# A graph layer on one core: the row that places and bins are compared with moves into a PSUM bank, and the counts get one PSUM buffer in place of two

## The chip, the cores and the metric

The kernel runs on one core of one Trainium2 chip. The metric is the device time of one execution in microseconds (us), the median of the runs shown. The engines are called PE (TensorE, matmuls; PEld is its weight load), DVE (VectorE), ACT (ScalarE), POOL (GpSimd) and SP (SyncE, which here only issues DMAs). SBUF is the on-chip memory of all engines, PSUM the memory in which PE leaves its sums[...].

## The reference

There are 12,500 nodes with 128 features and 400,000 edges, each with a source `src`, a destination `dst` (the edges are sorted by it), 20 attributes and a weight.

```
smu(v) = ((1 + a) * v + (1 - a) * v * erf(mu * (1 - a) * v)) / 2      a = 0.01, mu = 2.5

h    = relu(layernorm(x))
hf   = h @ W_in2f.T
Wij  = (smu(f_ij @ W_f1.T + b_f1) @ W_f2.T + b_f2) * edge_weight
x_ij = hf[dst] * Wij
agg  = segment_sum(x_ij, src, 12500)
out  = x + smu(agg @ W_o1.T + b_o1) @ W_o2.T + b_o2
```

So every edge reads the row of its destination, multiplies it with a filter made from its attributes, and is added to the row of its source. The sources are in no order.

## The kernel before

**Tiles.** The edges are cut into 3125 tiles of 128, four tiles make a group (782 groups; `GRP`), two groups share one set of loads (`load`, L366). The nodes are cut into `NB` = 98 bins of 128 by their source number. The groups come in seven parts (`PARTS`): six of 118 groups and one of 74. Each part has a buffer `buf` in HBM in which every bin has a fixed number of places.

**One group on its way.** PE multiplies the attributes with `w_f1` into `pu` (`hide`, L478), ACT applies Gelu (`ge`, L486), DVE makes `sm` of it (L494), PE multiplies with `w_f2` into `pw` (L528). DVE compares the edges' destinations with the partition number (`oh`, L386), and with this one-hot matrix PE gathers the destinations' rows from `hw` into `ph` (L509); ACT copies them to `hg` (L517), DVE multiplies `pw` and `hg` into `mt` (L538). PE turns `mt` into `pt` (L548), ACT scales it with the edge weight into the message buffer `ms` (L558, four instructions), of which there are six, and POOL stores the 128 rows of each tile into `buf` with one indirect DMA (L561): four for a group, 3125 in all. A buffer `ms` comes free when its stores have landed.

**Where a row goes.** The store needs each edge's place in its bin. `bins` (L392) has DVE compare the row 0, 1, 2, ... with the edges' bin numbers `hi_b`, giving `po` (128 edges x 4 tiles x 98 bins, L399), and add up the earlier tiles' in `co` (L410, L413). `count` (L419) has PE sum these down the edges into `pc` (L426, L427), and `read` (L447) has ACT pick each edge's number out of `pc` (L456, four instructions and their sums). `number` (L465) makes the index `ix` that the store uses.

**Adding up.** While a part is stored, the part before it is summed: SP loads places of two bins at a time into `rw` (L582), `choose` (L586) has DVE compare the row 0, 1, 2, ... with the number inside the bin that each place carries, giving the one-hot matrix `se` (128 places x 12 x 128, L593), and `add` (L597) has PE multiply it with the places into `pg` (L606), which DVE adds to `agg` (L619). The last part is summed after the last store, together with the output layers (`half`, L320, and `rest`, L332). Part 0 has nothing to sum; in its place the remaining node rows are normed and multiplied with `w_in` (`rows_of_h`, L185).

**The order.** In the loop over groups (L678) the order on PE, DVE, ACT and SP is the order in which the lines stand (`manual_schedule`): in the round of group g the steps `turn(g)`, `send(g)`, `number(g+1)`, `weigh(g+1)`, `gather(g+1)`, `take(g+1)`, half of the sums, `mix(g+1)`, `hide(g+2)`, `bend(g+2)`, `count(g+2)`, `read(g+2)`, `smooth(g+2)`, every other round `pick`, `bins(g+3)`, and the rest of the sums. Nobody overtakes on an engine. The sums begin in the fifth round of a part (`WAIT` = 4), and `choose` for the first bins stands before the third.

The row 0, 1, 2, ... is kept twice in SBUF: `irow` as float32, made by POOL (L113), and `irow_b` as bfloat16, copied from it (L116). PSUM is full in the loop: two buffers each for `pc` and `pg`, one each for `pu`, `ph`, `pw` and `pt`.

Of the kernel before, what the change touches and what calls it, by code (L numbers as in the profile page):

```python
# [9 lines left out]
F32 = mybir.dt.float32  # L10
BF = mybir.dt.bfloat16
# [8 lines left out]
P = 128  # L20
# [9 lines left out]
GRP = 4  # L30
# [9 lines left out]
def gnn_kernel(  # L40
# [19 lines left out]
    nc = tc.nc  # L60
# [4 lines left out]
    NB = (N + P - 1) // P  # L65
# [10 lines left out]
    for n in PARTS:  # L76
        n = min(n, left)
# [7 lines left out]
    for a, n in eps_of:  # L85
# [9 lines left out]
    const = ctx.enter_context(tc.tile_pool(name="const", bufs=1))  # L95
# [17 lines left out]
    irow = const.tile([P, P], F32, name="irow")  # L113
    nc.gpsimd.iota(irow, pattern=[[1, P]], base=0, channel_multiplier=0,
                   allow_small_or_imprecise_dtypes=True)
    irow_b = const.tile([P, P], BF, name="irow_b")  # L116
    nc.vector.tensor_copy(irow_b, irow)

    tri = const.tile([P, P], F16, name="tri")
    lift = const.tile([P, P], F32, name="lift")  # L120
# [97 lines left out]
    with tc.tile_pool(name="prep", bufs=1) as prep, \  # L218
# [44 lines left out]
        for a, m in chunks(NT // P, GRP) + [(NT // P, 0)]:  # L263
# [8 lines left out]
            elif NT % P:  # L272
                m = NT % P
# [71 lines left out]
    with tc.tile_pool(name="ld", bufs=4) as ld, \  # L345
# [4 lines left out]
            tc.tile_pool(name="ps2", bufs=2, space=PSUM) as ps2, \  # L350
            tc.tile_pool(name="ps1", bufs=1, space=PSUM) as ps1, \
            tc.manual_schedule(engines={ET.PE, ET.DVE, ET.Activation, ET.SP}):
        NF = 4
        fbufs = []
        for i in range(NF):
            fb = ld.tile([P, SUP * P], F32, name=f"f{i}", bufs=1)
# [9 lines left out]
        def load(s):  # L366
# [3 lines left out]
            e0, n = t0 * P, nt * P  # L370
            fb = fbufs[s % NF]
            nc.sync.dma_start(fb[0:R, :n], f_t[:, e0:e0 + n])
# [19 lines left out]
        def bins(g):  # L392


            if g >= NG:
                return
            t, n = groups[g]
            po = cnt.tile([P, GRP, NB], F16, name="po")
            nc.vector.tensor_tensor(po[:, :n], irow_b[:, :NB].unsqueeze(1).to_broadcast([P, n, NB]),  # L399
                                    hi_b[:, t:t + n].unsqueeze(2).to_broadcast([P, n, NB]), op=ALU.is_equal)  # L400
            co = cnt.tile([P, GRP + 1, NB], F16, name="co")
            if g in first:
                k = first[g]
                nc.vector.memset(co[:, 0], 0.0)
                m = sum(groups[i][1] for i in range(g, min(g + eps_of[k][1] * PER, NG)))
                begins[k] = (t, cnt.tile([P, max(n for _, n in eps_of) * SUP], F32, name="hic", bufs=2))
                nc.vector.tensor_scalar(begins[k][1][:, :m], hi_b[:, t:t + m], float(CAP[k]), None, op0=ALU.mult)
            else:
                pl, cl, nl = last.pop(0)
                nc.vector.tensor_add(co[:, 0], cl[:, nl - 1], pl[:, nl - 1])  # L410
            more = g + 1 in first or g + 1 in (NG, BY)
            for j in range(1, n + more):
                nc.vector.tensor_add(co[:, j], co[:, j - 1], po[:, j - 1])  # L413
            last[0] = (po, co, n)
            bins_of[g] = (po, co)
# [3 lines left out]
        def count(g):  # L419

            if g >= NG:
                return
            n = groups[g][1]
            po, co = bins_of.pop(g)
            pc = ps2.tile([P, GRP, NB], F32, name="pc")
            nc.tensor.matmul(pc[:, :n], ones_h, co[:, :n], start=True, stop=False)  # L426
            nc.tensor.matmul(pc[:, :n], tri, po[:, :n], start=False, stop=True)  # L427
            counts[g] = pc
            if g + 1 == BY:
                pt = ps1.tile([P, GRP * P], F32, name="ph")[:, :NB]  # L430
                nc.tensor.matmul(pt, ones_h, co[:, n], start=True, stop=True)
                mm = cnt.tile([P, 2], F32, name="mm")
                nc.vector.tensor_reduce(mm[:, 0:1], pt[:, :NB - 1], op=ALU.max, axis=AX.X)
                nc.vector.tensor_scalar(bad[:, 3:4], mm[:, 0:1], float(ZMIN[0]), None, op0=ALU.is_gt)
            if g + 1 in first or g + 1 == NG:

                k = epoch[g // PER]
                pt = ps1.tile([P, GRP, P], F32, name="ph")[:, 0, :NB]
                nc.tensor.matmul(pt, ones_h, co[:, n], start=True, stop=True)
                mm = cnt.tile([P, 2], F32, name="mm")  # L440
                nc.vector.tensor_reduce(mm[:, 0:1], pt, op=ALU.max, axis=AX.X)
                nc.vector.tensor_reduce(mm[:, 1:2], pt[:, :NB - 1], op=ALU.min, axis=AX.X)
                i = 4 + 2 * k
                nc.vector.tensor_scalar(bad[:, i:i + 1], mm[:, 0:1], float(CAP[k]), None, op0=ALU.is_gt)
                nc.vector.tensor_scalar(bad[:, i + 1:i + 2], mm[:, 1:2], float(ZMIN[k]), None, op0=ALU.is_lt)
# [140 lines left out]
        def choose(k, c):  # L586

            b = c * SPAN[k]
            if b >= NB:
                return  # L590
            m = min(SPAN[k], NB - b) * Q[k]
            se = rowp.tile([P, ROWS, P], F32, name="se", bufs=2)
            nc.vector.tensor_tensor(se[:, :m], irow.unsqueeze(1).to_broadcast([P, m, P]),  # L593
                                    rows_in[c][:, :m, P:P + 1].to_broadcast([P, m, P]), op=ALU.is_equal)
            sel[c] = se

        def add(k, b, q):  # L597

            g = b % GRP
            c, i = b // SPAN[k], b % SPAN[k]  # L600
            if q == 0 and g == 0:
                pgs[0] = ps2.tile([P, GRP, P], F32, name="pg")
            if q == 0 and i == 0:
                choose(k, c + 1)
            o = i * Q[k] + q
            nc.tensor.matmul(pgs[0][:, g, :], rows_in[c][:, o, 0:P], sel[c][:, o, :], start=(q == 0),  # L606
                             stop=(q == Q[k] - 1))
            if q < Q[k] - 1:
                return
            if i == SPAN[k] - 1 or b == NB - 1:  # L610
                rows_in.pop(c), sel.pop(c)
                fetch(k, c + AHEAD)
            if g == GRP - 1 or b == NB - 1:
                dst = agg[:, (b - g) * P:(b + 1) * P]
                src = pgs[0][:, :g + 1].rearrange("p b n -> p (b n)")
                if k == 0:
                    nc.vector.tensor_copy(dst, src)
                else:
                    nc.vector.tensor_add(dst, dst, src)  # L619
# [18 lines left out]
        for g in range(3):  # L638
            bins(g)
        count(0)  # L640
        read(0)
        count(1)
        read(1)
        number(0)
# [33 lines left out]
        for g in range(NG):  # L678
# [24 lines left out]
            if k and i == WAIT - 2:  # L703
                choose(k - 1, 0)
# [14 lines left out]
            hide(g + 2)  # L719
            bend(g + 2)  # L720
            count(g + 2)
            read(g + 2)
            smooth(g + 2)
            if g % PER == 0:
                pick((g + 4) // PER)
            bins(g + 3)
            parts(k - 1, hi)
            step()
            assert k == 0 or next(h_steps, None) is None
        k = EPOCHS - 1  # L730
        begin(k)
        choose(k, 0)
        mids, ends = [], []
        units_in = {}
# [169 lines left out]
```

## Time and profile before

| what | value |
|---|---|
| median of 3 runs | 4601.06 us (4593.67 to 4603.17) |
| the profiled execution, its own time | 4605.67 us |
| its span, from the first to the last instruction | 4603.9 us |
| mean granted clock of PE | 0.949 |
| DVE, `se` (L593), 128x1536 | 326 instructions, 1753 ns each |
| DVE, `po` (L399), 128x392 | 781 instructions, 559 ns each |
| DVE, `mt` (L538), 128x512 | 781 instructions, 748 ns each |
| ACT, reads of `pc` (L456) | 3125 instructions, 361 ns each, and as many of 226 ns that take the sums out |
| PE, sums of rows (L606) | 7840 instructions, 1109 us busy |
| first and last store (L561) | from 93.6 us; the last begins at 4405.8 us |

A group's row in the profile gives the line, the engine, the operation, what it writes and reads, and the number of instructions; then the busy time in us and the mean of one in ns; then the engine's idle time just before them and what ended most of it. A row of the timeline gives the start and the duration in us, the same names, and in square brackets the idle time before it with what ended it. A row of a wait gives who waited for whom: us in total, times, the longest. A float32 matmul shows as two instructions on PE. A stretch given in us counts from the start of the span.

### The profile page before, as it was taken

What the parts mean: (1) busy time and instruction counts of PE and PEld (TensorE: products, weight loads), DVE (VectorE), ACT (ScalarE), POOL (GpSimd) and SP (SyncE); (2) the same over time, 40 slices, a digit from 0 to 9 for tenths busy, and PEclk for the clock granted to TensorE, in tenths of its full rate; (3) what the DMA queues carried; (4) which work ended last, traced back from release to release, by engine and by line L of the source; (5) the groups of instructions that cost most, each with busy time, mean ns of one, the idle gap of its engine ahead of it and who ended that gap; (6) DMA issues with size and microseconds to landing.
All of it is one profiled execution on the core that took longest, in us unless ns stands there. A gap on an engine that the chain in (4) does not pass through costs nothing. (4 is left out here: it accounts for less than half of the span.)

```text
span 4603.9 us, 73307 instructions
## 1 busy us (share of the span) xinstructions
PE 3824.8 (83%) x18332; PEld 2340.7 (51%) x18596; DVE 3181.2 (69%) x8458; ACT 2809.9 (61%) x11054; POOL 3355.9 (73%) x3137
## 2 busy tenths in 40 slices
PE   4777787988879888879888878888798888799967
PEld 2334434555545555545555545555455555466656
DVE  5876676767667667757766767667576676687746
ACT  3776785666656666657666666666576666566500
POOL 1777777777777777777777777777777777777720
PEclk9999998999999999989999989999999999899978
DMA  6945565656646656646655556556465555466556
GB/s 187 212 139 169 157 167 173 193 174 184 181 131 214 190 175 183 181 145 206 190 180 172 168 171 199 172 179 186 125 209 173 169 172 166 138 197 183 164 179 175
DMA packets 457331, 808.84 MB, mean 176 GB/s; under 512 B 82228, under 2 KB 258630, under 8 KB 456512
## 3 DMA queue, kind: packets, MB, share of 16 engines
q1 hardware_dynamic: 328136, 573.65, 43.1%
q0 software_dynamic: 101504, 212.48, 14.2%
q10 hardware_dynamic: 27256, 17.94, 1.3%
q8 instruction: 147, 2.41, 0.2%
q14 instruction: 288, 2.36, 0.2%
HBM read 449.68 MB, written 354.07 MB: 175 GB/s over the span
## 5 line engine op out<-in xcount | busy, mean ns | idle before, releaser
L561 POOL DMA_INDIRECT buf<-ms,ix x3125 | 3349.1, 1072 | 1050.3 <-issue 268.7
L558 ACT ACTIVATE ms<-pt,w_sb 128x128 f32<-128x128 f32 x3125 | 903.2, 386 | 905.8 <-DMA buf<-ms,ix 699.8
L606 PEld LDWEIGHTS pg<-se,rw 128*128 128x128 f32 x7840 | 1087.1, 195 | 189.9 <-issue 51.7
L606 PE MATMUL pg<-se,rw 128*128 128x128 f32 x7840 | 1109.0, 278 | 35.7 <-DVE se L593 35.6
L456 ACT ACTIVATE jk<-pc,nbig 128x98 f32<-128x98 f32 x3125 | 1034.8, 361 | 12.3 <-PE pc L427 11.9
L548 PE MATMUL pt<-ident,mt 128*128 128x128 f32 x3125 | 512.8, 288 | 561.3 <-DVE mt L538 558.1
L528 PE MATMUL pw<-sm,w_f 128*128 128x512 f32 x1564 | 923.5, 674 | 27.1 <-DVE sm L494 21.6
L538 DVE SCALAR_TENSOR_TENSOR mt<-pw,b,hg 128x512 f32<-128x512 f32 x782 | 584.7, 748 | 514.6 <-ACT hg L517 511.3
L478 PE MATMUL pu<-f,w_f 128*128 128x512 f32 x1564 | 813.8, 602 | 2.6 <-DVE sm L494 2.5
L486 ACT ACTIVATE ge<-pu 128x512 f32<-128x512 f32 x782 | 472.9, 605 | 395.4 <-PE pu L478 360.2
L593 DVE TENSOR_TENSOR se<-irow,rw 128x1536 f32<-128x1536 f32 x327 | 572.6, 1751 | 193.0 <-DMA rw<-buf 159.5
L456 ACT ACTIVATION_READ_ACCUMULATOR jk<-pc,nbig 128x1 f32 x3125 | 705.0, 226 | 0.0
L548 PEld LDWEIGHTS pt<-ident,mt 128*128 128x128 f32 x3125 | 355.3, 145 | 668.5 <-DVE mt L538 664.1
L509 PE MATMUL ph<-oh,hw 128*128 128x512 bf16 (+1 forms) x2082 | 651.5, 396 | 16.1 <-issue 3.1
L494 DVE SCALAR_TENSOR_TENSOR sm<-pu,ge 128x512 f32<-128x512 f32 x782 | 535.6, 685 | 150.6 <-ACT ge L486 143.8
L517 ACT ACTIVATE hg<-ph 128x512 f32<-128x512 f32 x782 | 471.4, 603 | 210.2 <-PE ph L509 207.9
L413 DVE TENSOR_TENSOR co<-co,po 128x98 f16<-128x98 f16 x2351 | 503.7, 214 | 81.3
L509 PEld LDWEIGHTS <-hw 128*128 128x128 bf16 x2346 | 239.2, 102 | 585.9 <-issue 493.6
L399 DVE TENSOR_TENSOR po<-irow_b,hi_b 128x392 f16<-128x392 bf16 x782 | 436.8, 559 | 0.0
L555 DVE CAST ms<-lo_b 128x4 f32<-128x4 bf16 x782 | 150.6, 193 | 315.9 <-DMA buf<-ms,ix 312.8
L528 PEld LDWEIGHTS pw<-sm,w_f 128*128 128x128 f32 x1564 | 244.1, 196 | 165.7 <-DVE sm L494 163.1
L426 PE MATMUL pc<-co,ones_h 128*128 128x392 f16 x782 | 257.9, 330 | 13.3 <-DMA rbc<-rel_dram 12.8
(114 smaller groups left out, 1771.2 us busy)
## 6 DMA issues: line engine op xcount, KB each, us to landing
rw<-buf SPq DMA_DIRECT2D x326, 774.0 KB
buf<-zero SPq DMA_DIRECT2D x294, 387.0 KB
rbc<-rel_dram SPq DMA_DIRECT2D x390, 256.0 KB
buf<-ms,ix POOLq DMA_INDIRECT x3125
hw<-h_dram SPq DMA_DIRECT2D x391, 96.0 KB
f<-in_f_t SPq DMA_DIRECT2D x390, 80.0 KB
buf<-zero SPq DMA_DIRECT2D x49, 258.0 KB
h_dram<-hs SPq DMA_DIRECT2D x24, 384.0 KB
```

The costliest lines, as they stand in the source:

```text
L413: nc.vector.tensor_add(co[:, j], co[:, j - 1], po[:, j - 1])
L456: nc.scalar.activation(jk, pc[:, j], AF.Relu, bias=nbig, accum_out=sl[:, j:j + 1])
L478: nc.tensor.matmul(pu[:, :n], w_f1, loaded[g // PER][0][:, o:o + n], start=True, stop=True)
L494: nc.vector.scalar_tensor_tensor(sm[:, :n], units_of.pop(g)[:, :n], LIN, hidden[g][:, :n], op0=ALU.mult, op1=ALU.add)
L509: nc.tensor.matmul(ph[:, :n], hw[:, q * D:(q + 1) * D], oh[:, o:o + n], start=(q == 0), stop=(q == 2))
L528: nc.tensor.matmul(pw[:, :n], w_f2, hidden.pop(g)[:, :n], start=True, stop=True)
L538: nc.vector.scalar_tensor_tensor(mt[:, :n], pws.pop(g)[:, :n], b2, rows_of.pop(g)[:, :n], op0=ALU.add, op1=ALU.mult)
L548: nc.tensor.transpose(pt[:, j, :], mt[:, j * P:(j + 1) * P], ident)
L558: nc.scalar.activation(ms[:, j, 0:P], pt[:, j], AF.Copy, scale=w_sb[:, t + j:t + j + 1])
L561: i = nc.gpsimd.indirect_dma_start(out=bufs[k][:, :], out_offset=bass.IndirectOffsetOnAxis(ap=ix[:, j:j + 1], axis=0), in_=ms[:, j, :], in ...
L593: nc.vector.tensor_tensor(se[:, :m], irow.unsqueeze(1).to_broadcast([P, m, P]), rows_in[c][:, :m, P:P + 1].to_broadcast([P, m, P]), op=ALU ...
L606: nc.tensor.matmul(pgs[0][:, g, :], rows_in[c][:, o, 0:P], sel[c][:, o, :], start=(q == 0), stop=(q == Q[k] - 1))
```

## The change

The float32 row is copied once into a PSUM bank of its own (`irow_ps`), and `po` and `se` read it there. To free that bank, `pc` has one buffer in place of two, of four times 128 columns, of which 98 are used. The bfloat16 copy `irow_b` goes. The order of the steps in the loop is as before; apart from the new names and the shape of `pc`, only a few steps of the preparation trade places.

```diff
-    irow_b = const.tile([P, P], BF, name="irow_b")
-    nc.vector.tensor_copy(irow_b, irow)
...
             tc.manual_schedule(engines={ET.PE, ET.DVE, ET.Activation, ET.SP}):
+
+        irow_ps = ps1.tile([P, GRP * P], F32, name="irow_ps")[:, 0:P]
+        nc.vector.tensor_copy(irow_ps, irow)
...
             po = cnt.tile([P, GRP, NB], F16, name="po")
-            nc.vector.tensor_tensor(po[:, :n], irow_b[:, :NB].unsqueeze(1).to_broadcast([P, n, NB]),
+            nc.vector.tensor_tensor(po[:, :n], irow_ps[:, :NB].unsqueeze(1).to_broadcast([P, n, NB]),
                                     hi_b[:, t:t + n].unsqueeze(2).to_broadcast([P, n, NB]), op=ALU.is_equal)
...
-            pc = ps2.tile([P, GRP, NB], F32, name="pc")
+            pc = ps1.tile([P, GRP, P], F32, name="pc")[:, :, 0:NB]
             nc.tensor.matmul(pc[:, :n], ones_h, co[:, :n], start=True, stop=False)
...
             se = rowp.tile([P, ROWS, P], F32, name="se", bufs=2)
-            nc.vector.tensor_tensor(se[:, :m], irow.unsqueeze(1).to_broadcast([P, m, P]),
+            nc.vector.tensor_tensor(se[:, :m], irow_ps.unsqueeze(1).to_broadcast([P, m, P]),
                                     rows_in[c][:, :m, P:P + 1].to_broadcast([P, m, P]), op=ALU.is_equal)
```

## The prediction

> **What bounds the kernel now.** I read the page's busy table first, then the costliest groups, then the waits, then GpSimd's (POOL's) rows in order of time beside VectorE's (DVE's). In the table PE looks like the bound with 83%, and POOL has 73%:
>
> ```profile
> PE 3824.8 (83%) x18332; PEld 2340.7 (51%) x18596; DVE 3181.2 (69%) x8458; ACT 2809.9 (61%) x11054; POOL 3355.9 (73%) x3137
> ```
>
> The table misleads. The groups give the indirect stores 1072 ns each and 1050 us of idle time before them, and the waits say who stands behind them: ScalarE (ACT) waits 700 us for a store to land, because it wants the message buffer `ms` back.
>
> ```profile
> L561 POOL DMA_INDIRECT buf<-ms,ix x3125 | 3349.1, 1072 | 1050.3 <-issue 268.7
> ```
>
> ```profile
> ACT ms L558 <- DMA buf<-ms,ix: 699.8, 306, 20.1
> ```
>
> POOL in order of time, from 2048 us:
>
> ```profile
> 2048.62 0.96 POOL L561 DMA_INDIRECT buf<-ms,ix  x1 [0.30 <-ACT ms L558]
> 2049.89 1.69 POOL L561 DMA_INDIRECT buf<-ms,ix  x1 [0.30 <-issue]
> 2051.89 0.96 POOL L561 DMA_INDIRECT buf<-ms,ix  x1 [0.30 <-ACT jk L456]
> ...
> 2062.01 0.96 POOL L561 DMA_INDIRECT buf<-ms,ix  x1 [0.30 <-DVE co L410]
> 2063.28 1.97 POOL L561 DMA_INDIRECT buf<-ms,ix  x1 [0.30 <-issue]
> ```
>
> DVE in the same stretch:
>
> ```profile
> 2048.99 1.75 DVE L593 TENSOR_TENSOR se<-irow,rw 128x1536 f32<-128x1536 f32 x1
> ...
> 2062.67 1.75 DVE L593 TENSOR_TENSOR se<-irow,rw 128x1536 f32<-128x1536 f32 x1
> ```
>
> The reader is to see two things. First, the gap between two stores is always 0.30 us: it is the price of a step, not a wait. Over all 3125 rows only 13 us of gap lie above 0.305 us. So POOL works without a pause from 93.6 to 4406.8 us, and an undisturbed store costs 0.96 + 0.305 = 1.266 us, 5.07 us for a group of four. Second, two stores are long, and each ends 0.84 us after the end of a `se` (2048.99 + 1.75 = 2050.74, and 2049.89 + 1.69 = 2051.58; 2062.67 + 1.75 = 2064.42, and 2063.28 + 1.97 = 2065.25). A store that meets a `se` early in its life stands still until that `se` is over.
>
> I counted this over the trace. 597 of the 3125 stores are longer than 1.0 us, by 346 us in all above 0.961 us; 586 of them end 0.84 us after the end of a DVE row, to 20 ns. By that row: `se` (L593) 294 stores and 280 us, `po` (L399) 167 and 43 us, `oh` (L386) 70 and 10 us, the first `co` add (L410) 40 and 6 us, `hs` (L211) 13 and 5 us, others under 1 us. The other way round, by what DVE ran 90 ns after the start of a store: `se` held 294 of 307, `po` 179 of 202, `hs` 13 of 13; `mt` (L538) 0 of 292, `agg` (L619) 0 of 63, `sm` (L494) 10 of 432, by 0.1 us each. `se`, `po` and `hs` read two tensors of SBUF; `mt`, `agg` and `sm` read one of SBUF and one of PSUM. That is the whole of the case for the change: it turns `se` and `po` into the second kind.
>
> **The blocks: which rule.** The Trainium skill ("SBUF — State Buffer", "Who interferes with whom") says in my words that VectorE and GpSimd share one pair of SBUF ports as an exclusive lock, and that a VectorE instruction with two SBUF inputs contends with a GpSimd instruction that reads SBUF. But it goes on that tensor_tensor does not stall such stores: it takes "only the pair's read interface", and descriptors need the write interface (the page calls this inferred). By that sentence the change is worth 0 us. By the rows it is worth up to 280 + 43 = 323 us. I take the rows: 294 of 307 is no accident. (The rule is also too wide in one place: the f16 adds at L413 have two SBUF inputs and held 0 of 359.)
>
> **What is gained, part by part.** The edge groups come in seven parts of 118 groups (74 in the last), with first stores at 93.6, 726.6 and so on to 3986.6 us. POOL gains all of a block only where nothing else becomes the limit.
>
> Parts 1 to 5: `se` and `po` blocks sum to 52.4 + 55.0 + 50.3 + 55.1 + 52.7 = 265.5 us. The other engines can follow. After each part's start they run free of POOL for some twenty groups, because the message buffers are free there:
>
> ```profile
> 771.77 1.14 ACT L558 ACTIVATE ms<-pt,w_sb 128x128 f32<-128x128 f32 x4 [0.57 <-PE pt L548]
> ...
> 832.34 1.16 ACT L558 ACTIVATE ms<-pt,w_sb 128x128 f32<-128x128 f32 x4
> ```
>
> These rows are 13 groups apart: 60.6 / 13 = 4.66 us a group, against POOL's new 5.07 plus the `oh` blocks, 5.09. So 265 us.
>
> Part 0: it has no `se`. Its `po` blocks are 4.3 us before group 48 and 3.1 us after group 92. Between these, steps for the node rows slow the engines to (578.3 - 323.4) / 42 = 6.07 us a group, POOL waits for them, and 0.7 us of blocks gain nothing. So 7 us.
>
> Part 6: the same 588 sums of rows fall on 70 groups, not 114, and PE is nearly full:
>
> ```profile
> 2100.00:2600.00 500.00, 437.36 (x2133) 269.85 (x2161) 356.82 (x938) 322.37 (x1287) 389.72 (x363) 0.98 0.61 186
> 4000.00:4370.00 370.00, 349.66 (x1967) 240.44 (x2001) 294.63 (x708) 238.54 (x945) 292.62 (x255) 0.99 0.60 182
> ```
>
> (First the stretch and its length, then PE, PEld, DVE, ACT, POOL busy.) PE goes from 87% to 95%. The L558 rows of 30 groups here, from 3995.0 to 4148.9 us, give 5.13 us a group, above 5.07. POOL took 419.2 us; with 49.1 us of blocks gone it would need 370, but the engines need 71.25 x 5.13 plus two groups at 5.1, 375.7 us. So 43.5 us, and here PE is the next bound.
>
> After the last store (4406.8 us) come 197 us of sums and output in which POOL does nothing. `se` blocks nobody there, so nothing changes. Sum gained: 265.5 + 7.4 + 43.5 = 316 us.
>
> **What is added.** (a) The duration of `se` and `po`. Nearest rows: L337 adds PSUM and SBUF, 128x512, in 690 ns; L338 adds two SBUF tensors of that size in 692 ns. I take 0. Above: a row of PSUM read over and over has no row in this trace; see the rivals. Below: L619 has 683 ns, 9 ns less, x 327 = 3 us of DVE time that hides under POOL. (b) One `pc` in place of two: the count of group g+1 on PE now waits for ACT's four reads (L456) of group g, and behind it PE's sums of rows queue. In the trace the next count starts at least 1.95 us after the last of these reads (median 2.6), except once: the second count of all starts 0.97 us before. So 1 us at the start, and 0 later; the cover is the time that PE spends on `pt`, `pw`, `ph` and `pu` in between. Were the cover gone, 0.5 us a group would take 4.66 to 5.16 and cost 5 x 118 x 0.07 = 41 us. (c) `pc` is now written as four runs of 98 with gaps. The Trainium skill ("PSUM — Partial Sum Buffer", Specifications) says that a non-contiguous pattern slows matmuls significantly; no row here shows one. I take 0, since the run of 98 stays whole. Twice the price would be 0.33 us a group (L426 and L427 start 0.17 us apart): 4.99 in parts 1 to 5, still under 5.09, and 71 x 0.33 = 23 us in part 6. (d) One 128x128 copy into PSUM in place of one cast of 0.21 us; DVE then waits 1.90 us for a load anyway: 0. Moved steps in the preparation: 0, within 3 us either way. (e) At each part's start the engines' lead over POOL (from the last L558 row of a group to its first store) falls from some 23 to 2.3 us, then 4.1, 3.9; a faster POOL eats 0.3 to 0.5 us of it per group and may run dry for a moment: 6 x 0.5 = 3 us.
>
> Sum: 316 - 1 - 3 = 312 us. The profiled execution took 4605.7 us (span 4603.9 and 1.8 around it), so 4294; it lies 4.6 us above the median 4601.06, so 4289.
>
> **Rivals.** *PE binds in parts 1 to 5 too* (12%). For: PE's busy share would rise from 87% to 95%, which is where part 6 stands. At 5.2 us a group: 5 x 118 x (5.2 - 5.09) = 65 us, so 4354, up to 4390 with (c). Against: the 4.66 measured with both kinds of work running. *The change does not do what it says* (4%): the operand's place is not what blocks; then 4601. Against: 0 of 292 for `mt`. *Slower* (4%): DVE reads the repeated PSUM row at half pace. `se` would take 1.75 + 1.6 and `po` 0.56 + 0.41 us. DVE is busy 357 of 500 us, 3.9 of 5.5 us a group, and would need 3.9 + 0.67 + 0.41 = 5.0, and 0.65 us a group that it spends waiting for `hg` (511 us in all) does not shrink: 5.65 in parts 1 to 5, and 6.5 in part 6, where `se` comes more often; 94 + 118 x 5.4 + 590 x 5.65 + 74 x 6.5 + 197 and 33 x 1.6 for the tail gives 4795. It decides from about 0.5 us of added DVE time a group on.
>
> **How the numbers follow.** The likeliest case (80%) is 4289, in itself 4262 (no block at all left, 346 us, and no loss to PE but 7) to 4320 (PE's pattern cost in part 6 and a few us more). The range 4262 to 4350 takes in half of the first rival. A difference of 0.2%, 9 us, is about what a measurement of this kernel can tell. Faster 0.92, the same 0.04, slower 0.04.
>
> **What would show it.** Right: POOL's mean falls from 1072 to about 970 ns, long stores behind `se` and `po` vanish and those behind `oh` stay; `se` stays at 1.75 and `po` at 0.56 us; ACT's wait for the landing falls from 700 to about 400 us; the last store starts near 4090 us; 197 us follow it. Wrong: stores still end 0.84 us after a `se`, or gaps above 0.305 us appear in parts 1 to 5 (PE binds, and PE waits at L426 for the reads at L456), or `se` grows.

## The result and the profile after

| | before | after |
|---|---|---|
| median | 4602.11 us (4 runs, 4593.67 to 4607.44) | 4288.51 us (4 runs, 4284.47 to 4295.33) |
| the profiled execution, its own time | 4605.67 us | 4295.33 us |
| its span | 4603.9 us | 4293.6 us |
| first store begins, last store ends | 93.6, 4406.8 us | 93.5, 4095.8 us |
| after the last store | 197.1 us | 197.8 us |
| stores longer than 1.0 us | 597, by 346 us | 134, by 20 us |

The ratio is 0.9322, with a 95% interval of 0.9303 to 0.934. The whole difference lies between the first and the last store: that stretch is 311 us shorter, the span 310 us.

The first line of the busy table and the group of the stores after the change (the line numbers are one higher than before in this part of the code):

```profile
PE 3745.7 (87%) x18332; PEld 2305.2 (54%) x18596; DVE 3177.7 (74%) x8458; ACT 2825.2 (66%) x11054; POOL 3029.8 (71%) x3137
```

```profile
L562 POOL DMA_INDIRECT buf<-ms,ix x3125 | 3023.1, 967 | 1065.4 <-issue 278.4
```

DVE does the same work in the same time (3178 us, before 3181); its two changed instructions:

```profile
L594 DVE TENSOR_TENSOR se<-irow_ps,rw 128x1536 f32<-128x1536 f32 x326 | 570.6, 1750 | 162.0 <-DMA rw<-buf 135.8 <-PE pg L607 25.9 <-PE ph L510 0.2
L400 DVE TENSOR_TENSOR po<-irow_ps,hi_b 128x392 f16<-128x392 f32 x781 | 433.6, 555 | 0.0
```

POOL is shorter by 326 us in the same 3125 stores: 967 ns each in place of 1072. The gap between two stores is again 0.305 us; in parts 1 to 5, where hardly a gap is longer, POOL still sets the pace, although PE and DVE have larger shares in the table.

POOL in order of time, and below it the two `se` of DVE in the same stretch:

```profile
1947.40 1.04 POOL L562 DMA_INDIRECT buf<-ms,ix  x1 [0.30 <-ACT ge L487]
...
1950.05 0.96 POOL L562 DMA_INDIRECT buf<-ms,ix  x1 [0.30 <-issue]
1951.31 0.96 POOL L562 DMA_INDIRECT buf<-ms,ix  x1 [0.31 <-issue]
...
1960.17 0.96 POOL L562 DMA_INDIRECT buf<-ms,ix  x1 [0.30 <-issue]
1961.44 0.96 POOL L562 DMA_INDIRECT buf<-ms,ix  x1 [0.30 <-ACT jk L457]
```

```profile
1949.56 1.75 DVE L594 TENSOR_TENSOR se<-irow_ps,rw 128x1536 f32<-128x1536 f32 x1
...
1959.49 1.75 DVE L594 TENSOR_TENSOR se<-irow_ps,rw 128x1536 f32<-128x1536 f32 x1
```

The stores that begin at 1950.05 and 1960.17 us begin inside a `se`, as those of 2049.89 and 2063.28 us did before, and take 0.96 us where those took 1.69 and 1.97 us. By the same count as in the prediction (what DVE ran 90 ns after a store began): `se` held 0 of 384 stores, `po` 0 of 254; `oh` held 81 of 123, for 12 us.

### The profile page after: what moved, and what is told of

It reads as the page before. It is cut to its first block, busy times and chain, and to the rows that moved or that the text cites. A ratio compares the mean times of both kernels' runs of the same rounds, so it can differ in the third digit from the quotient of the medians.

```text
span 4293.6 us, 74022 instructions
## 1 busy us (share of the span) xinstructions
PE 3745.7 (87%) x18332; PEld 2305.2 (54%) x18596; DVE 3177.7 (74%) x8458; ACT 2825.2 (66%) x11054; POOL 3029.8 (71%) x3137
## 4 chain that ended last, share of the span: by engine, by line
PE 33%; DMA 15%; DVE 13%; ACT 5%; issue 3%; POOL 1%; ACTq 0%; DVEq 0%; POOLq 0%; SPq 0%
DMA buf<-ms,ix 13%; PE pw L529 8%; PE pg L607 8%; PE pu L479 6%; PE ph L510 5%; PE pt L549 4%; DVE se L594 4%; DVE mt L539 2%; DMA hg<-in_x 2%; ACT ms L559 2%; DVE sm L495 1%; ACT ge L487 1%; ACT jk L457 1%; DVE co L414 1%; DVE agg L620 1%
## 5 line engine op out<-in xcount | busy, mean ns | idle before, releaser
L562 POOL DMA_INDIRECT buf<-ms,ix x3125 | 3023.1, 967 | 1065.4 <-issue 278.4
L607 PEld LDWEIGHTS pg<-se,rw 128*128 128x128 f32 x7840 | 1075.3, 193 | 168.2 <-issue 23.4
L529 PE MATMUL pw<-sm,w_f 128*128 128x512 f32 x1564 | 897.5, 656 | 27.1 <-DVE sm L495 19.6
L549 PE MATMUL pt<-ident,mt 128*128 128x128 f32 x3125 | 497.6, 282 | 347.3 <-DVE mt L539 343.8
L594 DVE TENSOR_TENSOR se<-irow_ps,rw 128x1536 f32<-128x1536 f32 x327 | 571.8, 1749 | 162.0 <-DMA rw<-buf 135.8
L457 ACT ACTIVATION_READ_ACCUMULATOR jk<-pc,nbig 128x1 f32 x3125 | 682.9, 219 | 0.0
L510 PE MATMUL ph<-oh,hw 128*128 128x512 bf16 (+1 forms) x2082 | 635.2, 387 | 15.5 <-issue 2.0
L400 DVE TENSOR_TENSOR po<-irow_ps,hi_b 128x392 f16<-128x392 f32 x782 | 433.9, 555 | 0.0
L479 PEld LDWEIGHTS pu<-f,w_f 128*128 128x128 f32 x1564 | 250.4, 194 | 23.6 <-DVE sm L495 4.1
```

The costliest lines, as they stand in the source:

```text
L457: nc.scalar.activation(jk, pc[:, j], AF.Relu, bias=nbig, accum_out=sl[:, j:j + 1])
L479: nc.tensor.matmul(pu[:, :n], w_f1, loaded[g // PER][0][:, o:o + n], start=True, stop=True)
L510: nc.tensor.matmul(ph[:, :n], hw[:, q * D:(q + 1) * D], oh[:, o:o + n], start=(q == 0), stop=(q == 2))
L529: nc.tensor.matmul(pw[:, :n], w_f2, hidden.pop(g)[:, :n], start=True, stop=True)
L549: nc.tensor.transpose(pt[:, j, :], mt[:, j * P:(j + 1) * P], ident)
L562: i = nc.gpsimd.indirect_dma_start(out=bufs[k][:, :], out_offset=bass.IndirectOffsetOnAxis(ap=ix[:, j:j + 1], axis=0), in_=ms[:, j, :], in ...
```

## The experiments

**The two operands one at a time, and the PSUM buffer by itself: a first chip.** Two kernels put back one operand each, and a third makes only the change to `pc`. A fourth adds a float32 addition of two SBUF tensors behind every `po`.

```diff
 se in SBUF again (e1_po_only, from the changed kernel)
-            nc.vector.tensor_tensor(se[:, :m], irow_ps.unsqueeze(1).to_broadcast([P, m, P]),
+            nc.vector.tensor_tensor(se[:, :m], irow.unsqueeze(1).to_broadcast([P, m, P]),
 po in SBUF again (e2_se_only, from the changed kernel; irow_b made as before)
-            nc.vector.tensor_tensor(po[:, :n], irow_ps[:, :NB].unsqueeze(1).to_broadcast([P, n, NB]),
+            nc.vector.tensor_tensor(po[:, :n], irow_b[:, :NB].unsqueeze(1).to_broadcast([P, n, NB]),
 one buffer for pc alone (e3_pc_only, from the kernel before)
-            pc = ps2.tile([P, GRP, NB], F32, name="pc")
+            pc = ps1.tile([P, GRP, P], F32, name="pc")[:, :, 0:NB]
 an added float32 addition (e4_f32_add, from the changed kernel; ea and eb are set to 1 once)
+            ec = cnt.tile([P, 400], F32, name="ec")
+            nc.vector.tensor_add(ec[:, 0:392], ea[:, 0:392], eb[:, 0:392])
```

> The changed kernel, but se reads the row from SBUF again (po and pc stay as changed). Place theory (two SBUF inputs hold the stores, one SBUF and one PSUM input do not): the 280 us of blocks behind se come back and po's stay away; 4289 + 235 in parts 1 to 5 + about 40 in part 6 = about 4564 us, some 300 stores ending 0.84 us after the end of a se, none after a po. Rival (the gain came with the pc buffer or the order, not with the place of the operand): 4289 us.

> The changed kernel, but po reads the bfloat16 row from SBUF again (se and pc stay as changed). Place theory: po's blocks come back in parts 0 to 5, about 38 us, and in part 6 PE hides them: about 4327 us. Rival (se alone matters, since po is short): 4289 us. Rival (pc's buffer): 4289 us too, but then the run with se in SBUF would be at 4289.

> The kernel before with one part of the change alone: one pc buffer of four times 128 columns in place of two of four times 98. Place theory, with 1.95 us between the last read of pc and the next count: no difference, 4602 us within 5. Rival (the one buffer makes PE wait for ACT): slower, up to 40 us. Rival (the gain came from here): 4289 us.

> The changed kernel with one added float32 addition of two SBUF tensors, 128x392, behind each po (its result is not used). Place theory: it is po over again, 0.55 us, and holds the stores that meet it: 35 to 45 us more, 4325 to 4335 us, nine of ten stores that meet it held. Rival (what held the stores was something of the comparison itself, its stride of 0 or its bfloat16 operand): no store held, 4289 to 4300 us.

These four came to a chip on which the kernel before takes 5327 us (median of 19 runs), and there the times tell none of the theories apart: 5420 us (ratio 1.0151, 1.0092 to 1.0209), 5323 us (0.9985, 0.9949 to 1.0021), 5366 us (1.0045, 1.001 to 1.0081), and 5341 us for one run of the fourth. The longest waits of the first of them, there, and of the same kernel on another chip:

```profile
POOL buf L562 <- issue: 831.9, 2196, 7.1
PEld pt L549 <- DVE mt L539: 829.9, 287, 10.0
```

```profile
ACT ms L559 <- DMA buf<-ms,ix: 628.4, 268, 20.9
PEld pt L549 <- DVE mt L539: 607.2, 426, 22.5
```

On the first chip POOL waits up to 7 us for nothing that the profile shows, and the wait of ACT for a store to land is no longer among the longest: POOL's gaps above 0.305 us sum to 1004 us (13 us in the profile of before). The engines stop for some us at a time (in the second kernel ACT stands for 4.29 us before a `ms`, and the profile has no better reason for it than a count, L431, that `ms` does not read), and the stores are no longer the bound. So less held time is worth nothing there. The granted clock is lower too, 0.89 to 0.90 in these profiles and 0.95 to 0.97 in those of the other chips; whether that is a cause of the stops or comes of them, no run shows. Why that chip stops, and why the first kernel is 1.5% slower on it, stays open. Only the count of held stores can be used, and it says the same as everywhere: with `se` in SBUF, `se` held 177 of 188 stores and `po` 0 of 215; with `po` in SBUF, `po` held 211 of 221 and `se` 0 of 233; the added float32 addition, 558 ns long, held 206 of 235.

**The same on a sound chip.** The first three kernels once more, unchanged, on a chip where the kernel before takes 4607 us.

> The kernel with se from SBUF and po from PSUM once more, because on the first chip the kernel before took 5327 us and its stores stood still for other reasons for over 800 us. Place theory as before: about 4564 us; some 295 stores held behind a se for some 280 us. Rival: 4289 us.

> The kernel with se from PSUM and po from SBUF once more, for the same reason. Place theory: about 4327 us; some 170 to 200 stores held behind a po for some 43 us. Rival: 4289 us.

> The kernel before with one pc buffer alone once more, for the same reason. Place theory: 4602 us within 5. Rival (PE waits for ACT's reads): up to 40 us slower.

Measured: 4547.6 us with `se` in SBUF (ratio 0.9881, 0.9862 to 0.9901), 4347.9 us with `po` in SBUF (0.944, 0.9424 to 0.9455), 4608.7 us with one `pc` buffer alone (1.0005, 0.9992 to 1.0019). The stores of the three, in this order:

```profile
L562 POOL DMA_INDIRECT buf<-ms,ix x3125 | 3280.0, 1050 | 1058.6 <-issue 243.4
```

```profile
L565 POOL DMA_INDIRECT buf<-ms,ix x3125 | 3090.4, 989 | 1051.8 <-issue 288.9
```

```profile
L561 POOL DMA_INDIRECT buf<-ms,ix x3125 | 3338.4, 1068 | 1054.5 <-issue 258.6
```

The time goes with the mean of a store: 1068 ns with one `pc` buffer alone, 1050 with `se` in SBUF, 989 with `po` in SBUF and 967 in the changed kernel, for 4609, 4548, 4348 and 4289 us. `se` in SBUF brings back 294 held stores and 269 us; `po` in SBUF 222 and 55 us, and 72 and 15 us more behind the first `co` add that follows `po` at once. The gains add up: 1.2% and 5.6% are 6.8%, and both together gave 6.8%. The buffer gives and costs nothing, so the rival that looked for the gain there falls, and so does the one in which PE waits for ACT's reads. My 4564 us was 16 us too high and my 4327 us 21 us too low, mostly for one reason: blocks are not a fixed sum. With `se` gone, more stores meet a `po` (67 us more held time than in the changed kernel, where the trace of before had 43 + 6), and with `po` gone fewer meet a `se` (269, before 280).

**What kind of instruction holds a store.** Both from the changed kernel: the float32 addition's place is taken by a float16 one, and by the same at an odd first element.

```diff
 e5_f16_add
+            ec = cnt.tile([P, 400], F16, name="ec")
+            nc.vector.tensor_add(ec[:, 0:392], ea[:, 0:392], eb[:, 0:392])
 e6_f16_odd
+            nc.vector.tensor_add(ec[:, 1:393], ea[:, 1:393], eb[:, 1:393])
```

> The changed kernel with one added float16 addition of two SBUF tensors, 128x392, behind each po (result not used). In the trace of before the f16 adds of L413, two SBUF inputs too, held 0 of 359 stores. If a two-element-per-cycle addition does not hold stores: 0.35 us on DVE, no store held, 4289 to 4295 us. If any two SBUF inputs do (the rule as the skill words it): 20 to 30 us more.

> As the run with the added float16 addition, but its three operands start at an odd element[...]. If the pace decides whether stores are held: as the float32 addition, 4325 to 4335 us. If the type decides: no store held, 4289 to 4300 us. If it still takes 0.35 us the run tells nothing.

The float16 addition took 352 ns (the float32 one 558) and made 4318 us in one run. At the odd element it was to become as slow as the float32 one, but it took 359 ns (4316 us in one run), so that run tells nothing of the pace. The group, then a store of POOL and the addition that it meets:

```profile
L408 DVE TENSOR_TENSOR ec<-ea,eb 128x392 f16<-128x392 f16 x782 | 275.6, 352 | 0.0
```

```profile
1945.94 1.15 POOL L569 DMA_INDIRECT buf<-ms,ix  x1 [0.30 <-issue]
```

```profile
1945.91 0.36 DVE L408 TENSOR_TENSOR ec<-ea,eb 128x392 f16<-128x392 f16 x1
```

The addition ends at 1946.27, the store at 1947.09 us, 0.82 us later. It held 158 of 202 stores that met it. So a float16 addition holds stores too, and the expectation that it would not, taken from the adds at L413, falls. Of the 28 us by which its last store ends later, 19 us are longer stores (974 in place of 967 ns in the mean); most of the rest lies in part 0, which took 9 us more, 4 us of them held time. There DVE's added work probably meets engines that are the limit.

**Where another engine is the limit.** In part 6 half of the sums are left out in one kernel: of the six matmuls of a bin of part 5's buffer three, so half of that part's contributions are missing from the output. Two more kernels spread the node rows of part 0 and make `oh` without a hold; all three start from the changed kernel.

```diff
 e7_spread
             turn(g)
             send(g)
-            step()
+            if g < 46:
+                step()
 e9_less_sums
+            halved = k == EPOCHS - 2
+            if not halved or q < Q[k] // 2:
...
-                             stop=(q == Q[k] - 1))
+                             stop=(q == Q[k] - 1 or halved and q == Q[k] // 2 - 1))
 e8_oh_psum (one_ps is a 1 in the bank of irow_ps)
-            nc.vector.tensor_scalar(oh[:, :n], loaded[s][1][:, :n], pcol, None, op0=ALU.is_equal)
+            nc.vector.scalar_tensor_tensor(oh[:, :n], loaded[s][1][:, :n], pcol, one_ps.to_broadcast([P, n]),
+                                           op0=ALU.is_equal, op1=ALU.mult)
```

> The changed kernel without half of the sums of rows that lie in part 6: three of six matmuls for each bin of part 5's buffer are left out, so half of that part's contributions are missing. If PE is what limits part 6 (5.13 us a group against POOL's 5.07 to 5.1), part 6 becomes as fast as POOL: from 377 to 371 to 373 us, POOL's gaps above 0.305 us there fall from 7 us to under 1, and the lead over POOL, under 7 us in nearly all groups, grows to about 20. Rival (something else limits it, DVE or the loads of rows): the lead stays under 7 us.

> The changed kernel, in part 0 from group 46 on two steps of the node rows a round in place of three. In the changed kernel the engines need 6.07 us a group from group 48 to 92 there and POOL stands still for 20 us in all. Spread to group 114 they should need about 5.4, which the lead of 23 us covers: part 0 falls from 626 to about 606 us, 4269 us. Rival (the stop at the start of part 1 gives it back, since the lead is small when part 0 ends): 4285 to 4289 us.

> The changed kernel, with oh made by a comparison and a product with a 1 read from PSUM, in place of the comparison alone, which held 81 stores for 12 us. Place theory: oh takes about 1.2 us in place of 0.48 and holds none: up to 12 us less in parts 0 to 5, 4278 us. Rival (0.36 us more a group on DVE makes part 6, where PE and DVE are the limit, longer by about as much): 4289 us and up.

Half of the sums (one run, 4289.7 us): part 6, up to the start of its last store, took 370.8 us in place of 377.4, POOL's gaps above 0.305 us there fell from 7.0 to 0.1 us, and the engines' lead over POOL at its end rose from 3 to 23 us. The busy times of the stretch from 3720 to 4060 us (its length, then PE, PEld, DVE, ACT, POOL), of the changed kernel and of this one:

```profile
3720.00:4060.00 340.00, 328.13 (x1864) 227.94 (x1897) 281.59 (x680) 228.97 (x898) 253.92 (x264) 0.98 0.69 204
```

```profile
3720.00:4060.00 340.00, 307.33 (x1483) 183.60 (x1484) 300.20 (x733) 244.63 (x960) 258.67 (x268) 0.98 0.71 210
```

With 21 us less of PE, POOL stores 268 tiles in place of 264, while DVE and ACT are busier. PE is the limit there, for 7 us. The run's total does not show this: it is 5.6 us under the profiled execution of the changed kernel (4295.33 us), but no lower than that kernel's median (4288.51 us), and one run can't settle more.

Node rows spread: 4262.4 us (5 runs; ratio to the kernel before 0.9264, 0.9249 to 0.9279), against 0.9322 for the change. Part 0 took 600.3 us in place of 625.7, with 0.5 us of gaps in place of 20.5; part 1 took 599.1 (599.9 before), so nothing was given back. This version beats both kernels. I expected 606 us: the held time fell too, to 3.7 us in part 0 in place of 8.5, since `hs` (L209, two SBUF tensors) held 4 stores in place of 13.

`oh` without a hold: 4311.1 us (5 runs; 0.9373, 0.9357 to 0.9389), 23 us slower than the change.

```profile
L565 POOL DMA_INDIRECT buf<-ms,ix x3125 | 3004.0, 961 | 1104.4 <-issue 252.1 <-ACT jk L460 233.4 <-ACT ms L562 176.5
L389 DVE SCALAR_TENSOR_TENSOR oh<-rbc,pcol,irow_ps 128x1024 bf16<-128x1024 bf16 x391 | 496.8, 1271 | 2.2 <-DMA rbc<-rel_dram 1.3 <-DVE f L360 1.0
```

The stores reach 961 ns, none held by `oh`, and each of parts 1 to 5 gains 3 us (596.5 in place of some 599.6). But the idle time before them grows from 1065 to 1104 us: part 0 lost 25 us and part 6 10 us, where DVE's 0.8 us more per `oh` meets engines that are the limit. The rival held, and not only in part 6, which it named: part 0 lost more.

## Why the prediction was right

The bound was read from POOL's rows and not from the shares, and that carried the rest. Step by step, with the time from part to part of the profiled executions:

- *Parts 1 to 5*: forecast 265 us. They took 3259.9 us before and 2998.2 after: 262. A part now takes 599 to 600 us, four stores of 1.266 us for 118 groups (597.6) and 3 us of blocks.
- *Part 0*: forecast 7 us, measured 7.4 (633.1 to 625.7). The stretch in which the node rows limit the engines is as long as before. The held time of the part fell by 15 us, since stores behind the first `co` add came free too, but POOL's gaps grew from 12 to 20 us: as forecast, what is freed in that stretch gains nothing.
- *Part 6*: forecast 43.5 us with PE as the next bound at 5.13 us a group, measured 41.8 (419.2 to 377.4), at 5.17 to 5.18 us a group. The run with half of the sums shows that it is PE.
- *After the last store*: forecast no change, measured 0.7 us more.
- *Duration of `se` and `po`*: forecast 0; 1750 ns (before 1753) and 555 ns (559).
- *One `pc`*: forecast 1 us at the start. The second count now starts 0.05 us after the last read in place of 0.97 us before it, and the first store begins at 93.5 us: nothing is left of it. Elsewhere the next count starts at least 1.77 us after the last read, before and after the change (1.95 in the prediction passed over two rounds); the cover held.
- *`pc` in four runs of 98*: each of the two matmuls that write it takes 330 ns before and after. The line of the Trainium skill ("PSUM — Partial Sum Buffer", Specifications) on non-contiguous patterns does not show here.
- *The rule that spoke against*: that a tensor_tensor does not stall such stores, since it takes only the read interface (the Trainium skill, "SBUF — State Buffer", "Who interferes with whom"), is not what this kernel shows; `se` in SBUF alone costs 259 us (4547.6 against 4288.5). The sentence of the same page about two SBUF inputs agrees with the counts: `se` held 294 of 307 stores before and 0 of 384 after.

Two statements were off. ACT's wait for the landing was to fall from 700 to about 400 us and fell to 287, while ACT now waits longer for PE (for `pu` 460 us, before 360):

```profile
ACT ge L487 <- PE pu L479: 459.9, 610, 2.9
ACT ms L559 <- DMA buf<-ms,ix: 287.0, 178, 19.6
```

And the remark that the rule on two SBUF inputs is too wide, because the float16 adds at L413 held no store, was wrong: the longer float16 addition held 158 of 202. The adds at L413, of 98 elements and 0.21 us, hold stores as well, but are over too soon to take one past the 1.0 us at which the count begins. In the trace of before, the 15 stores that begin 40 to 60 ns after such an add take 0.988 us in the median and end 0.83 us after its end. After the change the `co` add at L411, of the same size, took 17 of 87 stores past 1.0 us, by 0.05 us each.

The forecast of 4289 against 4288.51 us is closer than its steps: 312 us were forecast and 310 measured in the profiled executions; parts 1 to 5 were 3.8 us and part 6 1.7 us too high, against 4 us of small losses, at the first count and at the starts of the parts, that did not show (gaps of 0.1 us in each of parts 1 to 5). That these cancelled is luck, and so is the last step: the 4.6 us between the profiled execution and the median were 6.8 us after the change, where the profiled execution was the slowest of the four.

## What to carry to other kernels

Look at the engine whose idle time before each step is always the same: it may be the bound at 73% busy, and what lengthens its steps is then worth its full price. Where POOL issues indirect stores, give VectorE's long two-tensor instructions one operand in PSUM, if a bank can be had and its second buffer has a measured cover. And sum the gain part by part, with the pace that the other engines show where they run free: that names the next bound before the change is made.

## What the runs showed of the hardware that was not expected

- On one chip the kernel before takes 5327 in place of 4602 us, over 19 runs. There less held time is worth nothing (0.9985 with `se` in PSUM and `po` in SBUF, which on a sound chip gave 0.944): POOL's gaps sum to some 1000 us above 0.305 us each, and the stores are no longer the bound. The same source can have another bottleneck on another chip.
- The busy time of an instruction does not fix how many stores it holds: `po`, with the row in SBUF, held 167 stores before the change, 185 with one `pc` buffer alone and 222 with `se` in PSUM.
- A comparison of one bfloat16 SBUF tensor with a number (`oh`, 1024 elements in 0.50 us) holds stores as well: 81 of 123. Made by another instruction, in 1.27 us and with an operand in PSUM, it holds none.
